# A decoder layer on one core: seven-product values, rows in place for one expert slot, and a reordered passage from attention to the experts

## The chip, the core and the metric

The kernel runs on one core of a Trainium2 chip. Five engines work side by side: TensorE (PE in the profile) multiplies matrices into PSUM, VectorE (DVE) and ScalarE (ACT) do elementwise work, GpSimd (POOL) does elementwise work and issues the indirect DMAs, SyncE (SP) issues most other DMAs. Each engine works through its own instructions in a fixed order and waits on semaphores for the others. The metric is device time in microseconds, lower is better.

## The reference

The input is x, 16 batches of 256 tokens of 256 features, and a context of 77 tokens for each batch. All is float32. Three residual steps, each followed by a layernorm, make up the layer:

```python
# 1. recurrent step: h = silu(causal conv of 4 taps (x @ in_w.T + in_b)), 512 features
xp  = h @ xp_w.T + xp_b
a   = exp(-exp(xp[..., :16]))
b   = silu(xp[..., 16:]) * sum(h, axis=-1, keepdims=True)
state_t = state_{t-1} * a_t + b_t                  # a scan over 256 tokens, 16 states
x   = layernorm(x + states @ out_w.T + out_b)

# 2. attention of x over [layernorm(context) ; layernorm(x)], 8 heads of 128
ln  = layernorm(x) * g + b
kv  = concat([layernorm(context) * g' + b', ln]) @ Wkv + bkv   # 333 rows, keys and values
out = softmax((ln @ Wq + bq) * 128**-0.5 @ k.T) @ v
x   = layernorm(x + out @ Wo + bo)

# 3. experts: each of 4096 tokens picks 2 of 8; an expert takes at most 512, first come first served
weights = softmax over the two best scores of x @ expert_embeddings.T
final[tokens of e] += weight * (relu(tokens @ W1[e].T) @ W2[e].T)
x   = layernorm(x + final)
```

## The kernel before, in words

**Loop over heads.** The main loop (L919 to L928) goes over 16 batches b of 8 heads h, and three heads are in work at once. `head_kq` makes keys (`pk`) and queries (`pq`) of the new head; `head_out` (L507) multiplies the turned weights of the head two back with the values (`po`); `head_softmax` (L473) makes the scores `s`, their negated maximum `nm` on DVE, `exp` on ACT and the scaled `pn` on DVE; `head_turn` (L492) turns `pn` of the head one back on PE (`pa`, `pb`) and copies it to `ptt`.

**Steps.** What belongs to other batches is hung on heads of this loop through a table, `steps[b, h]`, filled by `at` (L691 on). For batch b+1 these are the pieces of the recurrent step (`rec_in`, `rec_state`, `rec_add`, `rec_out`), its second layernorm and transposition (`prep_norm`, `prep_keys`) and its values (`prep_values`, L434). For batch b-1 they are the output product `project` (L526), the transposition `turn_tokens` (L559), scores and choice of experts (`score_experts`, `choose`), and `dispatch` (L635), which writes each token's row, with its weights and places, into a table of rows `xg` in device memory through indirect DMAs of POOL, two per 128 tokens. Batch 0's pieces run in a prologue ahead of the loop. A planner of the framework fixes the order of instructions on each engine from the code and the tile buffers, so the order on an engine is not that of the source alone.

**Values.** Values are 256 by 1024 from 256 by 256: four 128x512 results in PSUM, each of two accumulated 128x512 products (`pv`, L443), so eight products a batch; two results are copied by DVE (L451), two by ACT (L453). General PSUM tiles (`bank`, tag "mm": `pv`, `ph`, `pw`, `px`, `pt`, `pi`, `pf` and others) share two buffers; `pk`, `pq`, `pa` and `po` have one each.

**Layernorm.** `layernorm` (L135) takes statistics on DVE and the root on POOL as a power (`rsqrt`, L130). `again` (L151) derives the factor of a layernorm of an already normalised tensor by a short string on POOL (`u`, `u2`, `u3`, then `rsqrt`). Two such strings are in each batch: `rlz` for `prep_norm`'s `zl`, `rlo` for `settle`'s output `o`.

**Experts.** There are nine slots. Slot 0 is the first 512 rows of expert 0, slot 1 the rows of expert 0 that come from the last batch (256 places), slots 2 to 8 are experts 1 to 7 with 512 rows each. `Rows` (L774) loads a slot's rows `xe` from `xg` (L782) and works out on DVE, from `dw` (L787) on, each row's weight, where its token's other expert left a result, and where its output goes. `turn_rows` turns the rows on PE (`pe`), `first_product` makes `pi` and relu on ACT (L844), `second_product` makes `pf`, scaled by the weight on ACT and stored to `oe_d`. A token is completed by the later of its two slots: `gather` (L868) fetches the earlier result by indirect DMA, `finish` (L880) adds, normalises (root by POOL) and writes the output rows by indirect DMA (L903).

**The passage.** For the last batch, 15, nothing follows in the loop, so its project, router and dispatch stand behind the loop. Slot 0's rows need only batches up to 14, slot 1's need batch 15.

Of the kernel before, what the change touches and what calls it, by code (L numbers as in the profile page):

```python
# [10 lines left out]
F32 = mybir.dt.float32  # L11
# [7 lines left out]
P = 128  # L19
# [19 lines left out]
def decoder_layer(  # L39
# [66 lines left out]
    ebase_last = cpool.tile([P, GT, E], F32, tag="ebase_last", name="ebase_last")  # L106
# [8 lines left out]
    oob, tok1 = part[:, 0:1], part[:, 1:2]  # L115
    oobs = cpool.tile([P, 2], F32, tag="oobs", name="oobs")
# [63 lines left out]
    emb_s = wpool.tile([P, DC, E], F32, tag="emb", name="emb_s")  # L180

# [77 lines left out]
    zero = wpool.tile([P, 2 * DX], F32, tag="zero", name="zero")  # L259
    G.memset(zero, 0.0)  # L260

    def clear(i):

        xg_z = xg.rearrange("(i p r) d -> i p (r d)", p=P, r=2)
        for j in range(2 * i, min(2 * i + 2, xg_z.shape[0])):
            nc.sync.dma_start(xg_z[j], zero)
# [12 lines left out]
    def rec_in(pr, c):  # L279

        if c == 0:
            hss[pr] = aw.tile([P, NI, PT], F32, tag="hs", bufs=2, name=f"hs{pr}")
            sums[pr] = aw.tile([P, PT], F32, tag="sums", bufs=2, name=f"sums{pr}")
        ph = bank(f"ph{pr}_{c}")
        for k in range(DC):
            T.matmul(ph, lhsT=inw[:, k, c * P : (c + 1) * P], rhs=xTs[pr][:, k, :], start=(k == 0), stop=(k == DC - 1))  # L286
        hp = a2.tile([P, PB, KC - 1 + S], F32, tag="hp", name=f"hp{pr}_{c}")
        G.memset(hp[:, :, 0 : KC - 1], 0.0)
        A.activation(
            hp[:, :, KC - 1 :], ph.rearrange("p (b s) -> p b s", b=PB), AF.Identity, bias=inb[:, c : c + 1]  # L290
        )
        cv = a2.tile([P, PB, S], F32, tag="cv", name=f"cv{pr}_{c}")
        V.tensor_scalar(cv, hp[:, :, 0:S], cw[:, c, 0:1], cb[:, c : c + 1], ALU.mult, ALU.add)
        for k in range(1, KC):
            V.scalar_tensor_tensor(cv, hp[:, :, k : k + S], cw[:, c, k : k + 1], cv, ALU.mult, ALU.add)  # L295
        z = cv.rearrange("p b s -> p (b s)")
        th = a2.tile([P, PT], F32, tag="th", name=f"th{pr}_{c}")
        A.activation(th, z, AF.Tanh)
        V.scalar_tensor_tensor(hss[pr][:, c, :], th, 1.0, z, ALU.add, ALU.mult)
        if c > 0:  # L300
            G.tensor_tensor(sums[pr], hss[pr][:, 0, :] if c == 1 else sums[pr], hss[pr][:, c, :], ALU.add)

    def rec_state(first, last):
# [20 lines left out]
        for b, r in zip(members, rows):  # L324
            T.matmul(sg[r, 0:S], lhsT=half, rhs=sums[b // PB][:, tokens(b)], start=True, stop=True)
# [19 lines left out]
    def rec_add(b):  # L345

        pys = [bank(f"py{b + i}") for i in range(PB)]
        for h in range(2):
            for i in range(PB):
                ys, w = yss[b + i]  # L350
                T.matmul(
                    pys[i][:, h * D : (h + 1) * D], lhsT=ys[:, h * P : (h + 1) * P], rhs=w, start=True, stop=True
                )
        for i in range(PB):
            y = b2.tile([P, 2, D], F32, tag="ya", name=f"ya{b + i}")
            V.tensor_tensor(
                y.rearrange("p h d -> p (h d)"), pys[i], xts.pop(b + i).rearrange("p h d -> p (h d)"), ALU.add
            )
            ysums[b + i] = y
            if b + i + 2 < B:  # L360
                load_x(b + i + 2)

    def rec_out(b):

        xs[b] = xpool.tile([P, 2, DX], F32, tag="xs", name=f"xs{b}")
        stats[b] = layernorm(xs[b], ysums.pop(b), 2, P, f"a{b}")

# [4 lines left out]
    def context(t):  # L372

        rows = ctx_rows(t)
        zc = b2.tile([P, 1, D], F32, tag="zc", name=f"zc{t}")
        layernorm(zc, ctxs[t].unsqueeze(1), 1, rows, f"c{t}")
# [57 lines left out]
    def prep_values(b, n):  # L434

        if n == 0:
            vs[b] = b2.tile([P, 3, INNER], F32, tag="v", name=f"v{b}")
            nc.sync.dma_start(vs[b][0:M, 2, :], vc_d[b * M : (b + 1) * M, :])
        jc, half = divmod(n, 2)
        pv = bank(f"pv{b}_{n}")  # L440
        f0 = half * 512
        for k in range(DC):
            T.matmul(  # L443
                pv,
                lhsT=kvts[b][:, k, jc * P : (jc + 1) * P],
                rhs=wkv_s[:, k, INNER + f0 : INNER + f0 + 512],
                start=(k == 0),
                stop=(k == DC - 1),
            )
        if half == 0:  # L450
            V.tensor_copy(vs[b][:, jc, f0 : f0 + 512], pv)  # L451
        else:
            A.copy(vs[b][:, jc, f0 : f0 + 512], pv)  # L453

    kts, qts, pns, ptts = {}, {}, {}, {}
# [36 lines left out]
    def head_turn(b, h):  # L492

        pn = pns.pop((b, h))
        pt01 = bank(f"pa{b}_{h}", "pa", 1)
        pt2 = bank(f"pb{b}_{h}", "po", 1)
        for jc, (j0, jn) in enumerate(JCS):
            for ic in range(2):
                c0 = (jc % 2) * S + ic * P
                dst = pt01 if jc < 2 else pt2  # L500
                T.transpose(dst[0:jn, c0 : c0 + P], pn[:, ic, j0 : j0 + jn], ident)  # L501
        ptt = b2.tile([P, 3, S], F32, tag="ptt", name=f"ptt{b}_{h}")
        V.tensor_copy(ptt[:, 0:2, :], pt01.rearrange("p (j i) -> p j i", j=2))  # L503
        A.copy(ptt[0:M, 2, :], pt2[0:M, 0:S])  # L504
        ptts[b, h] = ptt

# [17 lines left out]
    pws, norms = {}, {}  # L524

    def project(b, i):  # L526

        ot = outs_t[b]
        if i == 0:
            pws[b] = bank(f"pw{b}")  # L530
        for h in range(H):
# [6 lines left out]
            )  # L538
        if i == 0:
            return  # L540
# [5 lines left out]
        norms[b] = layernorm(xs[b], y, 2, P, f"b{b}")  # L546

# [9 lines left out]
    x2s, lgs, chosen = {}, {}, {}  # L557

    def turn_tokens(b):  # L559
        x2s[b] = b1.tile([P, DC, S], F32, tag="x2", name=f"x2{b}")  # L560
# [74 lines left out]
    def dispatch(b):  # L635
# [13 lines left out]
        if b == B - 2:  # L649
            V.tensor_copy(ebase_last, ebase)  # L650
            for t in range(GT):
                V.tensor_scalar(
                    ebase_last[:, t, 0:1], carry[:, 0:1], -1.0, float(CAP), ALU.mult, ALU.add
                )
# [8 lines left out]
        V.tensor_tensor(place, cum, ebase_last if b == B - 1 else ebase, ALU.add)  # L663
# [26 lines left out]
    steps = {(b, h): [] for b in range(B) for h in range(H)}  # L690

    def at(b, h, f, *args):
        if 0 <= b < B:
            steps[b, h].append((f, args))
# [4 lines left out]
    for b in range(B):  # L699
        nb = b + 1  # L700
        new_pair = nb % PB == 0 and nb < B
        if b > 0:
            early = int(b == B - 1)
            at(b, 2, project, b - 1, 0)
            at(b, 3, project, b - 1, 1)
# [5 lines left out]
        if new_pair:  # L711
# [9 lines left out]
            for n, h in enumerate((4, 5, 6, 7)):  # L721
                at(b, h, prep_values, nb, n)
        elif nb < B:
            at(b, 0, prep_norm, nb)
            at(b, 0, prep_keys, nb)
            for n, h in enumerate((1, 4, 5, 6)):
                at(b, h, prep_values, nb, n)
# [4 lines left out]
    for nb in range(4, B, 4):  # L732
        for i in range(2):
            at(nb - 3 + i, 0, load_xT, nb // PB + i)
            for c in range(NI):
                at(nb - 3 + i, (1, 3, 5, 7)[c] if i == 0 else 4 + c, rec_in, nb // PB + i, c)
# [16 lines left out]
    for n in range(4):  # L753
        prep_values(0, n)
# [9 lines left out]
    e0 = e2 = es = None  # L764
# [7 lines left out]
    rows, xets = {}, {}  # L772

    class Rows:  # L774


        def __init__(self, e):
            expert, r0, self.n = SLOTS[e]
            code = float(E - expert)
            self.x = x = e0.tile([P, NS, DX], F32, tag="xe", bufs=3, name=f"xe{e}")  # L780
            x = x[:, 0 : self.n, :]
            nc.sync.dma_start(x, xg[r0 : r0 + self.n * P, :].rearrange("(s p) d -> p s d", p=P))  # L782
            narrow = lambda tag, e, dtype=F32: es.tile([P, NS], dtype, tag=tag, name=f"{tag}{e}")[:, 0 : self.n]
            first, token = x[:, :, D + 3], x[:, :, D + 2]

# [27 lines left out]
            self.to = narrow("to", e, I32)  # L813
            V.tensor_tensor(self.to, to, late, ALU.add)
# [31 lines left out]

    def second_product(e, it):
        y = e2.tile([P, NS, D], F32, tag="ye", name=f"ye{e}")
        w2 = w2_s[SLOTS[e][0]]
        for s in range(SLOTS[e][2]):  # L850
            po = bank(f"pf{e}_{s}")
            for f in range(NF):
# [6 lines left out]
                )  # L859
            A.activation(y[:, s, :], po[:, 0:D], AF.Copy, scale=rows[e].w[:, s : s + 1])  # L860
            if s % 2 == 1 and e < LAST:
# [4 lines left out]
    gs = {}  # L866

    def gather(e):  # L868
# [3 lines left out]
        for s in range(R.n):  # L872
            G.indirect_dma_start(
# [4 lines left out]
            )  # L878

    def finish(e, y):  # L880
        R, g = rows.pop(e), gs.pop(e, None)
# [3 lines left out]
        for a, z in [(0, 2), (2, 3), (3, 4)] if e == LAST else [(a, a + 2) for a in range(0, R.n, 2)]:  # L885
            for s in range(a, z):
                c = slice(s, s + 1)
                u = es.tile([P, D], F32, tag="u", name=f"ue{e}_{s}")
                V.tensor_tensor(u, R.x[:, s, 0:D], y[:, s, :], ALU.add)
                if e > 0:  # L890
                    V.scalar_tensor_tensor(u, g[:, s, :], R.joins[:, c], u, ALU.mult, ALU.add)
# [7 lines left out]
            r = rsqrt(v, n, P, f"e{e}_{a}")  # L899
# [15 lines left out]
    for i in range(len(heads) + 2):  # L915
# [3 lines left out]
        if i == len(heads) - 1:  # L919
            rows[0] = Rows(0)  # L920
# [8 lines left out]
        if 1 <= i <= len(heads):  # L929
            head_turn(*heads[i - 1])  # L930
# [8 lines left out]
    turn_rows(0)  # L939
# [4 lines left out]
    for e in range(LAST + 1):  # L944
        it = first_product(e)
        if e < LAST:
            rows[e + 1] = Rows(e + 1)
            turn_rows(e + 1)
        y = second_product(e, it)
        if e < LAST:  # L950
            gather(e + 1)
        finish(e, y)
# [52 lines left out]
```

## Time and profile before

| what | value |
|---|---|
| median of 3 runs | 1219.05 us (1216.42 to 1219.24) |
| the profiled execution's own time | 1219.84 us |
| its span, first to last instruction | 1218.1 us |
| mean granted TensorE clock | 0.988 |
| PE, DVE, ACT, POOL busy | 1169.6, 719.1, 480.5, 304.4 us |
| heads of attention | about 85 to 1060 us |
| last `pf` starts | 1198.40 us |
| last output store issued by POOL | 1213.94 us |

A line of the groups view gives line, engine and operation, output and input tiles, shape and count, then busy time in us and mean ns of one, then the idle time of that engine just before, with what ended it. In the timeline, a line begins with start and duration in us, and brackets at its end give idle time before and what released it. A line of the list of waits gives the waiting instruction, what it waited for, the total in us, how many times, and the longest. A line of the table by stretches gives the length, then PE, weight loads, DVE, ACT and POOL busy, the granted clock, the share of the DMA engines and GB/s. A float32 product shows as two matmul records.

### The profile page before, as it was taken

Reading aid. Unit: us, or ns where it says so; the run is one execution under the profiler, and the core shown is the slowest. Engines: PE = TensorE matmul, PEld = TensorE weight load, DVE = VectorE, ACT = ScalarE, POOL = GpSimd, SP = SyncE. Lnnn points to the kernel's source line nnn. Section 1 sums busy time; section 2 is a strip of 40 time slices with the busy share of each in tenths; the row PEclk is TensorE's granted clock in tenths of the full one; section 3 lists DMA queues with packets and bytes.
Section 4 is the critical chain, followed back from the end, with each engine's and each line's share of the span. In section 5 each row is a group of like instructions: output and inputs, shape, how many; then the busy total and the mean of one; then the engine's idle time right before and its main releaser. Section 6 shows DMA issues by size and latency. Waiting matters only on the chain.

```text
span 1218.1 us, 15598 instructions
## 1 busy us (share of the span) xinstructions
PE 1169.6 (96%) x5146; PEld 836.7 (69%) x5146; DVE 719.1 (59%) x2108; ACT 480.5 (39%) x1261; POOL 304.4 (25%) x516
## 2 busy tenths in 40 slices
PE   6799999999999999999999999999999999889995
PEld 2347676767777767677777676677787778756663
DVE  6525667485645675766465757754556464555654
ACT  2134534353434343543343444434443344323331
POOL 3300232122211321122112311321122112135666
PEclk9899999999999999999999999999999999999998
DMA  6740101001000100010001010000010000045762
GB/s 226 241 156 0 36 20 36 20 31 33 20 19 24 35 28 14 10 53 9 14 10 31 10 31 9 24 9 14 9 48 9 13 10 12 21 146 134 189 163 84
DMA packets 43321, 60.89 MB, mean 50 GB/s; under 512 B 7596, under 2 KB 31116, under 8 KB 43240
## 3 DMA queue, kind: packets, MB, share of 16 engines
q1 hardware_dynamic: 36376, 50.40, 13.0%
q0 software_dynamic: 6144, 9.48, 3.1%
q8 instruction: 41, 0.67, 0.2%
q14 instruction: 40, 0.33, 0.1%
q10 hardware_dynamic: 720, 0.01, 0.0%
HBM read 36.60 MB, written 30.78 MB: 55 GB/s over the span
## 4 chain that ended last, share of the span: by engine, by line
PE 83%; DVE 9%; POOL 3%; issue 2%; DMA 2%; ACT 1%; POOLq 0%; SPq 0%; DVEq 0%; ACTq 0%
PE po L514 12%; PE pk L463 11%; PE s L478 10%; PE pw L532 9%; PE pq L468 8%; PE pv L443 8%; PE pi L837 4%; PE pa L501 4%; PE ph L286 4%; PE pf L853 3%; PE pvc L395 3%; PE pb L501 2%; DVE cv L295 2%; PE pl L574 1%; POOL xg L679 1%
## 5 line engine op out<-in xcount | busy, mean ns | idle before, releaser
L480 DVE TENSOR_REDUCE nm<-s 128x2 f32<-128x666 f32 x128 | 108.5, 848 | 139.8 <-PE s L478 139.8
L514 PE MATMUL po<-ptt,v 128*128 128x256 f32 (+1 forms) x768 | 190.9, 382 | 0.0
L514 PEld LDWEIGHTS po<-ptt,v 128*128 128x128 f32 (+1 forms) x768 | 143.7, 191 | 52.7 <-issue 30.6
L463 PE MATMUL pk<-kvt,wkv_s 128*128 128x333 f32 x512 | 165.1, 444 | 0.0
L478 PE MATMUL s<-kt,qt 128*128 128x333 f32 x512 | 164.4, 442 | 0.0
L484 ACT ACTIVATE p<-s,nm 128x333 f32<-128x333 f32 x256 | 135.3, 535 | 38.0 <-DVE nm L480 37.1
L522 ACT ACTIVATE ot<-po,bkv_s 128x256 f32<-128x256 f32 x128 | 60.8, 475 | 211.8 <-PE po L514 211.1
L468 PE MATMUL pq<-kvt,wq_s 128*128 128x256 f32 x512 | 131.2, 378 | 0.0
L443 PE MATMUL pv<-wkv_s,kvt 128*128 128x512 f32 x256 | 121.5, 599 | 0.0
L504 ACT COPY ptt<-pb 77x256 f32<-77x256 f32 x128 | 47.1, 368 | 179.8 <-PE pb L501 179.8
L478 PEld LDWEIGHTS s<-kt,qt 128*128 128x128 f32 x512 | 96.4, 189 | 31.3 <-ACT qt L470 0.5
L468 PEld LDWEIGHTS pq<-kvt,wq_s 128*128 128x128 f32 x512 | 96.7, 189 | 30.6 <-issue 0.5
L532 PE MATMUL pw<-wo_s,ot 128*128 128x256 f32 x512 | 117.6, 382 | 0.0
L532 PEld LDWEIGHTS pw<-wo_s,ot 128*128 128x128 f32 x512 | 97.5, 191 | 13.4 <-ACT ot L522 0.2
L463 PEld LDWEIGHTS pk<-kvt,wkv_s 128*128 128x128 f32 x512 | 87.6, 191 | 23.0
L489 DVE TENSOR_SCALAR pn<-p,rs 128x333 f32<-128x333 f32 x256 | 92.3, 396 | 4.2
L501 PEld LDWEIGHTS pa<-ident,pn 128*128 128x128 f32 x512 | 63.7, 141 | 35.7 <-DVE pn L489 7.4
L543 POOL TENSOR_TENSOR xb<-xs,bo_s 128x256 f32<-128x256 f32 x32 | 21.2, 686 | 268.0 <-DVE yb L545 268.0
L679 POOL DMA_INDIRECT xg<-xs,sidx x64 | 66.4, 1037 | 86.2 <-DVE sidx L676 71.6
L503 DVE COPY ptt<-pa 128x512 f32<-128x512 f32 x128 | 87.3, 682 | 0.7 <-PE pa L501 0.7
L501 PE MATMUL pa<-ident,pn 128*128 128x128 f32 x512 | 77.9, 274 | 4.4 <-DVE pn L489 4.4
L295 DVE SCALAR_TENSOR_TENSOR cv<-hp,cw,cv 128x512 f32<-128x512 f32 x96 | 72.5, 757 | 1.6
(174 smaller groups left out, 1588.9 us busy)
## 6 DMA issues: line engine op xcount, KB each, us to landing
v<-vc SPq DMA_DIRECT2D x16, 308.0 KB
vc<-vc SPq DMA_DIRECT2D x9, 512.0 KB
xg<-zero SPq DMA_DIRECT2D x17, 262.0 KB, 4.8
xe<-xg SPq DMA_DIRECT2D x8, 524.0 KB, 4.6
xT<-in_xT SPq DMA_DIRECT2D x8, 512.0 KB, 3.7
xt<-in_x_in SPq DMA_DIRECT2D x16, 256.0 KB, 2.9
out<-o SPq DMA_DIRECT2D x16, 256.0 KB, 2.1
w<-in_w1T SPq DMA_DIRECT2D x8, 512.0 KB
```

What stands on the lines that cost most here:

```text
L295: V.scalar_tensor_tensor(cv, hp[:, :, k : k + S], cw[:, c, k : k + 1], cv, ALU.mult, ALU.add)
L443: T.matmul(pv, lhsT=kvts[b][:, k, jc * P : (jc + 1) * P], rhs=wkv_s[:, k, INNER + f0 : INNER + f0 + 512], start=(k == 0), stop=(k == DC - 1),)
L463: T.matmul(pk[:, 0:J], lhsT=wkv_s[:, k, f], rhs=kvt[:, k, :], start=(k == 0), stop=(k == DC - 1))
L468: T.matmul(pq[:, 0:S], lhsT=wq_s[:, k, f], rhs=kvt[:, k, 0:S], start=(k == 0), stop=(k == DC - 1))
L478: T.matmul(s[:, ic, 0:J], lhsT=qt[:, ic * P : (ic + 1) * P], rhs=kt, start=True, stop=True)
L480: V.tensor_reduce(nm, s[:, :, 0:J], AX.X, ALU.max, negate=True)
L484: A.activation(p[:, ic, :], s[:, ic, 0:J], AF.Exp, bias=nm[:, ic : ic + 1], accum_out=sm[:, ic : ic + 1])
L489: V.tensor_scalar(pn[:, ic, :], p[:, ic, :], rs[:, ic : ic + 1], None, ALU.mult)
L501: T.transpose(dst[0:jn, c0 : c0 + P], pn[:, ic, j0 : j0 + jn], ident)
L503: V.tensor_copy(ptt[:, 0:2, :], pt01.rearrange("p (j i) -> p j i", j=2))
L514: T.matmul(po[:, 0:S], lhsT=vs[b][0:jn, jc, h * DH : (h + 1) * DH], rhs=ptt[0:jn, jc, :], start=(jc == 0), stop=(jc == 2),)
L532: T.matmul(pws[b][:, i * D : (i + 1) * D], lhsT=ot[:, h, i * P : (i + 1) * P], rhs=wo_s[:, h, :], start=(h == 0), stop=(h == H - 1),)
```

## The change

- **Values by seven products.** The 2x2 block product (two token halves, two feature halves of the inner dimension, two halves of the values) is formed from seven 128x512 products. The weight side needs four sums, made once on DVE (`weight_sums`). The token side needs four 128x128 sums a batch, made on POOL (`prep_sums`, behind `prep_keys`). Steps come at three heads. At each a first product (at the first step two) goes into a bank, is copied or added into the values, and later in the same head, behind `head_turn`, a second product is accumulated into the same bank and evicted again (`late_steps`, `behind`). Per batch 2 copies on ACT and 5 adds on DVE stand for 2 and 2 copies.
- **Recurrent step.** For the first pair of batches the sum over features is accumulated by PE over four blocks, without the sums on POOL. `rec_add` adds into the loaded input tile; the next load of x is asked for in `rec_out`. The context is normalised in place. `rec_in` of later pairs hangs on other heads. Clearing `xg` takes 34 DMAs of half the size.
- **The passage.** In batch 15 the steps of batch 14 come one head earlier and both halves of its project at head 2. Slot 0's rows are asked for one head earlier, turned behind the last head's turn, and their DVE work (`read`) is placed behind the last copy of `head_turn`. project(15) uses two banks, and each half is normalised as it comes (`norm_half`).
- **Slot 1 in place.** All 256 tokens of batch 15 are slot 1, in their own order, whether they chose expert 0 or not. `dispatch` gives them their places through `slot_last`; `turn_tokens` writes their transposed rows straight to slot 1's tile; no rows are loaded back, turned or gathered for it. `read_last` gives weight 0 and no output to tokens that are not expert 0's.
- **Finishing.** Slots 1 to 8 take the root by a Sqrt on ACT, a reciprocal and a Newton step on DVE (`root`). In slot 8 the input and the gathered result are added up ahead of the second product, whose PSUM result is then scaled and added by DVE. The gather of slot 8 goes ahead of slot 7's stores on POOL.

```diff
-    def prep_values(b, n):
+    def weight_sums():
+        w = lambda k, half: wkv_s[:, k, INNER + half * 512 : INNER + (half + 1) * 512]
+        t = lambda i: wsum[:, i, :]
+        V.tensor_tensor(t(0), w(0, 1), w(0, 0), ALU.subtract)
...
+    def prep_sums(b):
+        x = lambda i, k: kvts[b][:, k, i * P : (i + 1) * P]
+        sums = b1.tile([P, 4, P], F32, tag="tsum", name=f"tsum{b}")
+        s = lambda i: sums[:, i, :]
+        G.tensor_tensor(s(0), x(1, 0), x(1, 1), ALU.add)
+        G.tensor_tensor(s(2), x(0, 0), x(1, 0), ALU.subtract)
+        G.tensor_tensor(s(1), s(0), x(0, 0), ALU.subtract)
+        G.tensor_tensor(s(3), x(0, 1), s(1), ALU.subtract)
+        tsums[b] = x(0, 0), x(0, 1), s(3), x(1, 1), s(0), s(1), s(2)
+    def prep_values(b, n, second):
...
+        if not second:
+            banks[b, n] = p = bank(f"pv{b}_{n}")
+            product(p, (1, 5, 7)[n], False)
+            if n == 0:
+                p6 = bank(f"pv6_{b}")
+                product(p6, 6, False)
+                A.copy(c(1, 0), p)
+                V.tensor_tensor(c(1, 0), c(1, 0), p6, ALU.add)
...
+            return
+        p = banks.pop((b, n))
+        product(p, (2, 3, 4)[n], True)
+        if n == 0:
+            A.copy(c(0, 0), p)
+        elif n == 1:
+            V.tensor_tensor(c(0, 1), c(1, 0), p, ALU.add)
         else:
-            A.copy(vs[b][:, jc, f0 : f0 + 512], pv)
+            V.tensor_tensor(c(1, 0), c(1, 0), p, ALU.add)
...
-            early = int(b == B - 1)
+            early = 2 * int(b == B - 1)
             at(b, 2, project, b - 1, 0)
-            at(b, 3, project, b - 1, 1)
+            at(b, 3 - early // 2, project, b - 1, 1)
...
             at(b, 3, prep_keys, nb)
-            for n, h in enumerate((4, 5, 6, 7)):
-                at(b, h, prep_values, nb, n)
+            at(b, 3, prep_sums, nb)
+            for n, h in enumerate((4, 6, 7)):
+                at(b, h, prep_values, nb, n, False)
+                behind(b, h, prep_values, nb, n, True)
...
+        first = ((1, 1), (1, 3), (1, 5), (1, 7)) if nb == 4 else ((0, 5), (0, 7), (1, 0), (1, 5))
+        at(nb - 4 + first[0][0], 0, load_xT, pr)
+        at(nb - 2, 0, load_xT, pr + 1)
+        for c, (b, h) in enumerate(first):
+            at(nb - 4 + b, h, rec_in, pr, c)
+        for c, h in enumerate((3, 4, 5, 7)):
+            at(nb - 2, h, rec_in, pr + 1, c)
...
+            if e == 1:
+                self.x = xs[B - 1]
+                return
...
+    def root(v, n, name):
+        q = es.tile([P, n], F32, tag="qe", name=f"qe{name}")
+        A.activation(q, v, AF.Sqrt)
+        i0 = es.tile([P, n], F32, tag="ie", name=f"ie{name}")
+        V.reciprocal(i0, q)
...
-        if i == len(heads) - 1:
+        if i == len(heads) - 2:
             rows[0] = Rows(0)
...
-            head_turn(*heads[i - 1])
+            turned = head_turn(*heads[i - 1])
+        if i < len(heads):
+            for f, args in late_steps[heads[i]]:
+                f(*args)
+        if i == len(heads) - 1:
+            turn_rows(0)
+        if i == len(heads):
+            with tc.issue_after(turned.ins):
+                rows[0].read(0)
...
         y = second_product(e, it)
-        if e < LAST:
-            gather(e + 1)
-        finish(e, y)
+        gathered = gather(e + 1) if 0 < e < LAST else None
+        if e == LAST - 1:
+            with tc.issue_after(gathered.ins):
+                finish(e, y)
+        else:
+            finish(e, y)
```

## The prediction

> **What bounds the kernel now.** I read the page's totals first, then its chain and its cost table.
>
> ```profile
> PE 1169.6 (96%) x5146; PEld 836.7 (69%) x5146; DVE 719.1 (59%) x2108; ACT 480.5 (39%) x1261; POOL 304.4 (25%) x516
> PE 83%; DVE 9%; POOL 3%; issue 2%; DMA 2%; ACT 1%; POOLq 0%; SPq 0%; DVEq 0%; ACTq 0%
> L443 PE MATMUL pv<-wkv_s,kvt 128*128 128x512 f32 x256 | 121.5, 599 | 0.0
> ```
>
> TensorE is busy for 96% of the span and owns 83% of the chain, and the value products that the change thins out are on it. How tight it is shows the list of what PE waited for, between 85 and 1040 us, which is nearly the whole attention loop:
>
> ```profile
> PE sg L325 <- POOL sums L301: 3.3, 4, 0.8
> PE ph L286 <- DVE x L566: 1.7, 3, 0.6
> PE px L315 <- DVE hs L299: 1.2, 3, 0.4
> PE pa L501 <- DVE pn L489: 0.6, 3, 0.2
> ```
>
> 6.8 us of waits in 955: PE work taken out there shortens the span, and anything that makes PE wait lengthens it. The 16 batches take 59.7 us each. Next the last of these waits, at batch 7, head 3, on three engines (start, duration, engine; in brackets the idle time before and its releaser). POOL first, then DVE, then PE:
>
> ```profile
> 552.80 0.71 POOL L132 TENSOR_TENSOR rb<-vb,nhalf 128x2 f32<-128x2 f32 x1 [0.64 <-DVE mva L141]
> 554.47 0.69 POOL L132 TENSOR_TENSOR ra<-va,nhalf 128x2 f32<-128x2 f32 x1
> 558.09 0.70 POOL L132 TENSOR_TENSOR rlz<-u3z,nhalf 128x2 f32<-128x2 f32 x1
> ```
>
> ```profile
> 558.83 0.35 DVE L415 TENSOR_SCALAR zl<-xs,rlz 128x256 f32<-128x256 f32 x1 [2.30 <-POOL rlz L132]
> ```
>
> ```profile
> 555.36 1.88 PE L443 MATMUL pv<-wkv_s,kvt 128*128 128x512 f32 x4
> 557.08 1.46 PE L514 MATMUL po<-ptt,v 128*128 128x256 f32 x6
> 559.87 0.84 PE L501 MATMUL pa<-ident,pn 128*128 128x128 f32 x4 [0.20 <-DVE pn L489]
> ```
>
> POOL works from 552.80 to 558.79 without a gap; DVE stands 2.30 us at zl for it; the softmax scaling pn is queued behind zl, and PE's pa waits for pn. The slack of this string of small operations is −0.2 us: it is already used up. Last, what PE waits for at the end of attention and in the first experts, and the granted clock there:
>
> ```profile
> PE pa L501 <- DVE pn L489: 3.8, 1, 3.8
> PE pe L822 <- DMA xe<-xg: 3.2, 1, 3.2
> ```
>
> ```profile
> 1060.00:1080.00 20.00, 18.90 (x74) 12.51 (x74) 7.51 (x31) 3.31 (x7) 2.94 (x7) 0.92 0.18 61
> 1080.00:1100.00 20.00, 16.69 (x66) 13.37 (x65) 11.46 (x71) 4.99 (x11) 11.70 (x12) 0.83 0.60 177
> ```
>
> ```profile
> 1090.89 1.12 PE L822 MATMUL pe<-ident,xe 128*128 128x128 f32 x4 [3.20 <-DMA xe<-xg]
> 1092.12 6.32 PE L837 MATMUL pi<-xet,w 128*128 128x256 f32 x16
> ```
>
> **The change, part by part.**
>
> *A, prologue.* Batch 0's values: seven products for eight, −0.9. Four weight sums on DVE, 128x512, about 0.65 each (the 128x512 copies took 0.68), in a stretch where PE already waits for DVE (6.5 us before pt at 48.7): 0 to +2.6, I take +1. The packed state sum gets 16 matmuls for 4, some +0.5 net of the 0.8 us wait on POOL that goes. Normalising the context in place removes one buffer's wait: 0 to −1, I take −0.8. Sum −0.2.
>
> *B, values in the loop.* The four passes above are two products and start 1.72 us before the next group: 0.86 us a product. 15 batches × 0.86 = −12.9.
>
> *C, the new wait.* The seven products need four 128x128 sums a batch on POOL. By the POOL rows of 1302 ns for 512 columns and 686 for 256, 128 columns cost 0.38, and 0.08 more where one uses the last. In the order of the changed kernel's instructions, in each odd batch b = 1, 3, ... 13 three of the four stand in POOL's queue between u3o and ra, so ra, uz, u2z, u3z, rlz come about 3 × 0.38 + 0.1 = 1.25 us later. Behind rlz wait DVE's two zl halves, and rs and pn of head 3 behind those, and PE's pa behind pn: the string above, with no slack. At b=3, 7, 11 (0.2 us short now) pa comes 1.45 late, at b=5, 9, whose filler ph moves elsewhere, about 1.4; b=13 has about 0.4 of slack, so 0.9; b=1 keeps its filler. 5 × 1.43 + 0.9 = 8.1, less the 0.6 that is there now: +7.5. If cover appears, +2; if the fourth sum slips in too, +10.
>
> *D, rec_in moved.* The 1.7 us of ph <- x go, as ph isn't next to turn_tokens any more: −1.7 (0 at worst). The sums waits stay.
>
> *E, small waits.* `choose` now follows the head's pn in DVE's order and its count product can come 0.2 late in some batches: +0.5. Evictions of the values wait on ACT and DVE (5 adds and 2 copies for 4 copies a batch), +0.2. Second products follow the first by po, s, pa and pb (1.30+1.12+0.65 = 3.07 us), more than an eviction of 0.6 to 1.5: nothing is late. The clears become 34 DMAs of half the size on SP, 17 more issues of under 0.5 us, all in batches 0 and 1, where SP has little else; load_x, moved to rec_out, lands 2.9 us after issue and has more than a batch. Both 0.
>
> *F, end of attention.* From the end of head 7's s (1051.9) to the end of the first slot's pf (1087.5) it is 35.6 us. The work in it, at full clock: pa, pb 0.65, two po 2.6, pw 6.9, transposes of tokens 0.9, router 1.4, pe 0.9, pi 7.0, pf 6.9 = 27.2. The rest is the 3.8 of pa (DVE stands at dw for the rows' DMA, ahead of pn), 1.1 of smaller waits and a halved clock. Now dw and what follows come after the last turn, and rows are asked for one head earlier (batch 14's dispatch also one earlier); project(15) is normalised in halves, each hidden by the first expert's products. I leave 1.6 us of waits: 28.8, so −6.8 (−4 to −8).
>
> *G, slot 1 in place.* No store and reload of the last batch's rows of expert 0 (now scatter to 1088.1, load 2.7), no pe(1). From the end of pf(0) to slot 2's pi it was 15.1 us. After: pi(1) and pf(1) at 256 columns each half of 6.9, pe(2) 0.87, = 7.8; slot 2's rows still wait for the last scatter and their own load: the counts' product to rows took 13.56 before (1044.05 to 1057.61), I take 12.9, and pe(2) is due 10.7 after it: +2.2. 10.0, so −5.1. [...] The row: 3.20 us of waiting, then 1.1 of transposes, and pi(1) took 6.32 for 3.45. My wait with its transposes is 3.1 us. By the row's own size it is warm, G −5.1; [...] pf(1) runs halved, G −1.7. I keep −5.1 and that end; −7 if rows come in time.
>
> *H, experts 2 to 8.* PE is full, 14.8 us each (7.0+0.9+6.9); root() puts a Sqrt on ACT, in order, ahead of relus that free PE's banks, waiting for DVE's ve. In slot 1 the first relu of slot 2 is some 0.5 late: +0.5. Later the rows are in time by 3 us or more: 0, up to +4. POOL, relieved of pow, only gains.
>
> *I, tail.*
>
> ```profile
> 1199.99 0.99 POOL L873 DMA_INDIRECT ge<-oe,at  x1 [0.30 <-issue]
> 1213.94 1.02 POOL L903 DMA_INDIRECT out<-oe,to  x1 [0.74 <-DVE oe L902]
> ```
>
> The last gather starts 8.6 us after pf(7) ended (1191.4), behind the stores of slot 7; now ahead of them, about 2.9 after. gather and input are added before the last product, so behind pf(8) (1205.4) remain an add from PSUM, statistics, Sqrt, four small DVE operations, scaling and a store: 0.5+0.4+0.2+0.2+0.3+0.6+0.4, with the handovers near 4.7 us to the last oe's end, which came 8.3 after: −3.5 (−1.5 to −5).
>
> Sum: −0.2 −12.9 +7.5 −1.7 +0.7 −6.8 −5.1 +0.5 −3.5 = −21.5. The profiled execution took 1219.84 (span 1218.1 and 1.7 around it): 1198.3. It lies 0.8 above the median of 1219.05, hence 1197.5.
>
> **The rivals.** *C is covered.* The string at rlz finds slack, as another order of POOL or the moved ph would give: the sum is −29, 1190. For: only 0.2 us is missing today. Against: POOL has no gap there, and three sums must go somewhere.
>
> *The expert stage turns on ACT and DVE.* Each root() holds the in-order ACT queue until DVE's statistics are there; 0.5 to 1 us in each of seven slots, plus a half-clock after G: +7 to +10, 1206. For: PE's two banks leave a relu 1.7 us. Against: ACT is busy only 6.7 of 20 us there. [...] the one load in the trace took 1.28. With a switch there and back for each of 16 roots it would be 41 us by the row [...]. The order of instructions has one added load, ahead of a wait of 2.5 us for slot 1's ve: 0 by the row[...].
>
> *Slower.* A bank held from first to second product: PE's general tiles have two, and the head between would find none. 45 second products in the loop; they decide the sign from 21.5/45 = 0.48 us each on; at 0.6 it is 1197.5 + 27 = 1224.5. For: at the first step two banks are taken at once. Against: the 3.07 us above.
>
> **How the numbers follow.** Forecast as summed 0.60; C covered 0.20; experts late 0.15; banks 0.05. The forecast's own ends (C from +2 to +10, G, I, F) make 1190 to 1204; the covered case and the late experts reach 1186 and 1207, where 0.2 is left out. About 0.3%, 3.7 us, is what a measurement tells from no change: faster 0.94, same 0.02, slower 0.04.
>
> **What would show it.** Right: value products 224 matmul records instead of 256; batch period near 59.3 with pa <- pn waits of 1 to 1.5 us at six heads 3 or 4; no pa wait over 1 us near 1040; pi(1) at 3.5 us; span end about 9 us after the last pf. Wrong, if pa <- pn stays below 2 us in all (then 1190), if waits for relus or pe appear in each slot, or if the second products show waits of their own.

## The result and the profile after

The changed kernel takes 1198.87 us (median of 4 runs, 1197.72 to 1201.09) against 1219.14 us (median of 4, 1216.42 to 1219.27): a ratio of 0.9841, 95% interval 0.9821 to 0.9861, or 20 us less. The profiled execution of the changed kernel took 1201.09 us with a span of 1199.3 us, the one before 1219.84 us with 1218.1, so the two traces differ by 18.8 us. The traced execution of the changed kernel is the slowest of its four.

To see where those went I cut both spans at the same five events on PE. The stages in us, worked out from the starts and durations of these instructions in the timeline of PE:

| stage | before | after | difference | predicted |
|---|---|---|---|---|
| prologue, to the first head's s | 87.40 | 92.37 | +4.97 | -0.2 (A) |
| loop, to the end of the last head's s | 964.74 | 956.64 | -8.10 | -6.4 (B to E) |
| to the end of pf of slot 0 | 35.55 | 27.47 | -8.08 | -6.8 (F) |
| to the start of pi of slot 2 | 14.91 | 9.69 | -5.22 | -5.1 (G) |
| to the end of pf of slot 8 | 102.87 | 104.83 | +1.96 | +0.5 (H) |
| to the end of the span | 12.63 | 8.30 | -4.33 | -3.5 (I) |

The total fits, and two of its terms do not: the prologue got longer by 5 us, and the loop hides two errors of mine that cancel. In the other runs that keep this prologue the first s comes at 89.25 to 92.65 us, so beside 87.40 its cost is 1.9 to 5.3 us, and this trace lies near the upper end. First the loop. The list of what PE waited for between 85 and 1030 us in the changed kernel:

```profile
PE po L564 <- DVE ptt L552: 6.3, 7, 1.2
PE sg L331 <- POOL sums L305: 2.9, 4, 0.8
PE pa L550 <- DVE pn L538: 2.6, 5, 0.5
PE ph L290 <- ACT v L496: 0.4, 1, 0.4
```

The waits of ph for x and of px for hs are gone, and a new one stands at the top. It comes seven times, once in each odd batch. Batch 7, head 3, is nearly at the same time as in the kernel before, and shows how. POOL in the changed kernel:

```profile
554.15 0.22 POOL L160 TENSOR_SCALAR u3o<-u2o 128x2 f32<-128x2 f32 x1
554.45 0.41 POOL L460 TENSOR_TENSOR tsum<-kvt 128x128 f32<-128x128 f32 x1
554.94 0.46 POOL L462 TENSOR_TENSOR tsum<-tsum,kvt 128x128 f32<-128x128 f32 x1
555.48 0.46 POOL L463 TENSOR_TENSOR tsum<-kvt,tsum 128x128 f32<-128x128 f32 x1
555.89 0.70 POOL L134 TENSOR_TENSOR ra<-va,nhalf 128x2 f32<-128x2 f32 x1
...
559.52 0.70 POOL L134 TENSOR_TENSOR rlz<-u3z,nhalf 128x2 f32<-128x2 f32 x1
```

DVE at the same place, first in the kernel before:

```profile
555.19 0.74 DVE L146 TENSOR_SCALAR xs<-ya,mva,ra 128x256 f32<-128x256 f32 x2
555.85 0.68 DVE L503 COPY ptt<-pa 128x512 f32<-128x512 f32 x1
```

and in the changed kernel:

```profile
556.63 0.74 DVE L148 TENSOR_SCALAR xs<-xt,mva,ra 128x256 f32<-128x256 f32 x2 [1.49 <-POOL ra L134]
557.28 0.68 DVE L552 COPY ptt<-pa 128x512 f32<-128x512 f32 x1
560.25 0.35 DVE L425 TENSOR_SCALAR zl<-xs,rlz 128x256 f32<-128x256 f32 x1 [2.29 <-POOL rlz L134]
```

And PE:

```profile
558.11 1.54 PE L564 MATMUL po<-ptt,v 128*128 128x256 f32 x6 [0.85 <-DVE ptt L552]
559.48 1.28 PE L527 MATMUL s<-kt,qt 128*128 128x333 f32 x4
561.29 0.85 PE L550 MATMUL pa<-ident,pn 128*128 128x128 f32 x4 [0.53 <-DVE pn L538]
```

Three sums on POOL put ra off from 554.47 to 555.89 and rlz from 558.09 to 559.52, by 1.42 and 1.43 us. DVE now waits for ra as well, at xs, and the copy ptt stands behind xs. So PE pays 0.85 us at po, which comes about 3 us ahead of pa, and another 0.53 at pa: 1.38 in all.

The passage from attention to the experts has lost most of its gaps, and the granted clock is 1.00 in both stretches, for 0.92 and 0.83 before (columns as before: length, the five engines' busy time, clock, DMA share, GB/s), with what PE waits for from 1025 us to the end:

```profile
1060.00:1080.00 20.00, 19.93 (x84) 13.93 (x82) 12.78 (x70) 5.56 (x13) 8.63 (x13) 1.00 0.45 142
1080.00:1100.00 20.00, 18.22 (x77) 13.21 (x78) 12.33 (x68) 7.62 (x15) 9.60 (x10) 1.00 0.62 174
```

```profile
PE pe L956 <- DMA xe<-xg: 1.8, 1, 1.8
PE pf L996 <- DVE ye L1004: 1.8, 1, 1.8
```

The first of the two waits is slot 2's rows (predicted 2.2). The second is new: the last product waits for a bank.

### The profile page after: what moved, and what is told of

Read it like the earlier page. It is cut to its first block, busy times and chain, and to the rows that moved or that the text cites. A ratio compares the mean times of both kernels' runs of the same rounds, so it can differ in the third digit from the quotient of the medians.

```text
span 1199.3 us, 15750 instructions
## 1 busy us (share of the span) xinstructions
PE 1152.6 (96%) x5134; PEld 827.8 (69%) x5134; DVE 748.6 (62%) x2226; ACT 485.4 (40%) x1273; POOL 312.3 (26%) x560
## 5 line engine op out<-in xcount | busy, mean ns | idle before, releaser
L512 PEld LDWEIGHTS pk<-kvt,wkv_s 128*128 128x128 f32 x512 | 91.1, 191 | 45.0 <-issue 22.0
L538 DVE TENSOR_SCALAR pn<-p,rs 128x333 f32<-128x333 f32 x256 | 97.8, 416 | 3.8
L514 ACT ACTIVATE kt<-pk,bkv_s 128x333 f32<-128x333 f32 x128 | 69.0, 539 | 19.9 <-PE pk L512 19.6
```

What stands on the lines that cost most here:

```text
L512: T.matmul(pk[:, 0:J], lhsT=wkv_s[:, k, f], rhs=kvt[:, k, :], start=(k == 0), stop=(k == DC - 1))
L514: A.activation(kt, pk[:, 0:J], AF.Identity, bias=bkv_s[:, h : h + 1])
L538: V.tensor_scalar(pn[:, ic, :], p[:, ic, :], rs[:, ic : ic + 1], None, ALU.mult)
```

## The experiments

All times below are medians; those of the kernel before, run beside each group, were 1218.64 to 1219.00. Stages are cut as in the table above. A median carries the prologue, whose length varies among executions (last section), so the stage that an edit aims at is given beside it. Theory: seven products are worth 0.86 us each batch, and the sums' place in POOL's queue gives part of it back. First rival: the waits belong to the split products and their evictions on DVE. For the passage and the tail the rivals were other parts of the same edit.

**Sums on DVE, and sums behind rlz.** Two ways to take the sums out of the way:

```diff
-        G.tensor_tensor(s(0), x(1, 0), x(1, 1), ALU.add)
+        V.tensor_tensor(s(0), x(1, 0), x(1, 1), ALU.add)
...
```

> The changed kernel with the four token-side sums of each batch on DVE instead of POOL; nothing else changed. Theory (the sums stand ahead of ra in POOL's queue and hold up xs, ptt, zl and pn on DVE): PE's waits for ptt and pn at the seven odd batches, 9.0 us in the changed kernel, fall below 2.5 us in all, and the time to 1190 to 1194. Rival (the waits come from the evictions of the split products on DVE): they stay near 9 us or grow by the added 60 operations on DVE, and the time is 1198 or more.

```diff
+        if b > 1 and b % 2 == 1:                      # in rec_out: rlz is made at once
+            r2s[b] = again(*stats.pop(b), f"z{b}")
...
+    def sums_behind(b):
+        with tc.issue_after(lasts[f"z{b + 1}"].ins):  # POOL: behind rlz
+            prep_sums(b)
...
-            at(b, 3, prep_sums, nb)
-            for n, h in enumerate((4, 6, 7)):
+            at(b, 4, sums_behind, nb)
+            for n, h in enumerate((5, 6, 7)):
```

> The changed kernel with the sums still on POOL, but in odd batches queued behind rlz (which is computed earlier for that), and the values of those batches at heads 5, 6 and 7 instead of 4, 6 and 7. Theory (it is the place in POOL's queue, not the engine): the 9.0 us of waits at odd batches go nearly all, time 1189 to 1192. Rival (evictions of the split products): the waits move with the products to heads 5 to 7 and the time stays at 1198.

On DVE: 1193.64 us, 5.2 less than the changed kernel; its loop takes 951.61 us for 956.64. Waits of 5.0 us remain (4.2 for ptt, 0.8 for pn), because the sums now stand on DVE ahead of ptt; more than the 2.5 I expected. Behind rlz: 1190.78 us (ratio to before 0.9776, 0.9760 to 0.9792), 8.1 less, with a loop of 947.81. What PE waited for between 95 and 1040 us in that run is down to this:

```profile
PE sg L335 <- POOL sums L309: 2.8, 4, 0.8
PE po L574 <- DVE ptt L562: 0.3, 1, 0.3
```

The split products and their evictions were all still there, so the rival falls. In batch 7 of that run POOL has ra and rlz ahead of the sums:

```profile
547.57 0.69 POOL L134 TENSOR_TENSOR ra<-va,nhalf 128x2 f32<-128x2 f32 x1 [0.93 <-DVE va L145]
...
549.86 0.69 POOL L164 TENSOR_TENSOR rlz<-u3z,nhalf 128x2 f32<-128x2 f32 x1
550.51 0.41 POOL L466 TENSOR_TENSOR tsum<-kvt 128x128 f32<-128x128 f32 x1
```

This edit also moves the values' first step from head 4 to head 5 and makes rlz earlier; the run alone doesn't part those from the order of the queue. The run on DVE, which moves neither, shows that 5.0 us of the loop go with the sums' leaving POOL.

**Eight products again.** Everything of the change kept but the values:

```diff
-                at(b, h, prep_values, nb, n, False)
-                behind(b, h, prep_values, nb, n, True)
+                at(b, h, prep_values, nb, n)          # prep_values, its steps and copies as before
...
-    wparts = weight_sums()
-    prep_sums(0)
```

> The changed kernel with the values of before (eight products, four copies, no sums on POOL or DVE), everything else of the change kept. Theory (a product is worth 0.86 us on PE, the sums cost 9.0 us by POOL's queue, and 1 to 2 us in the prologue): +12.9 - 9.0 - 1.5 = +2.4 us, 1200 to 1203. Rival (PE isn't the bound where the values are made, the seven products gained little): the time falls to about 1190.

1201.72 us, +2.85 against an expected +2.4. By the stages the agreement is in part chance. The loop is longer by 2.6 us (959.21), and that is what the seven products bring in it, net. The passage is longer by 2.4 us (12.04 to slot 2's pi, for 9.69): slot 2's rows came later in that execution (2.53 us of waiting, for 1.85), and slot 1's pf took 4.53 us for 3.62. Against these stand 3.6 us of a shorter prologue (first s at 88.81) and 0.8 in the last slots, so that the two traces differ by 0.6 us only. The length of single batches, from one head 0's s to the next in the timelines of PE, takes it apart:

| batch | before | eight products | changed | sums behind rlz |
|---|---|---|---|---|
| 3 | 58.80 | 58.75 | 59.35 | 57.88 |
| 7 | 58.79 | 58.75 | 59.35 | 57.87 |
| 12 | 56.05 | 56.04 | 55.19 | 55.18 |
| 13 | 58.28 | 58.23 | 58.82 | 57.88 |
| 14 | 56.04 | 56.04 | 55.18 | 55.18 |

In batches 12 and 14, which are even, seven products give 0.85 and 0.86 us, as the row of before said (0.86). In batches 3 and 7 the changed kernel is 0.6 us longer instead of 0.86 shorter. Over the seven odd batches the loss beside the eight-product kernel, 0.86 taken off, is 1.3 to 1.5 us each and 10.1 us in all. The eight-product loop itself is 5.5 us shorter than that of the kernel before (964.74): that is what the moved rec_in and the other edits in the loop bring, of which 3.1 us are waits that went (6.8 to 3.7 us); the other 2.4 are not assigned to a row.

**The prologue.** In the changed prologue PE reaches the first context products with a longer gap behind the fourth ph (16.41 to 21.99 us, before 17.32 to 19.95) with only small matmuls in it, and the products take longer:

```profile
18.56 0.44 PE L389 MATMUL pt<-ident,ctx 128*128 128x128 f32 x2 [2.16 <-ACT hp L293]
19.90 0.64 PE L319 MATMUL px<-hs,xpw 128*32 128x256 f32 x8 [0.90 <-ACT kvc L391]
21.00 1.06 PE L331 MATMUL sg<-hs,half 128*32 128x256 f32 x2 [0.46 <-ACT hp L293]
21.99 9.78 PE L405 MATMUL pvc<-wkv_s,kvc 128*128 128x512 f32 x16
```

Before they took 7.13. The granted clock is 0.50 from 22 to 26 us here and was 1.00 in the kernel before. Two experiments take edits of the prologue back, the first with one tile where the kernel before had two:

```diff
-        zc = ctxs[t].unsqueeze(1)
-        layernorm(zc, zc, 1, rows, f"c{t}")
+        zc = b2.tile([P, 1, D], F32, tag="zc", bufs=1, name=f"zc{t}")   # before: two buffers
+        layernorm(zc, ctxs[t].unsqueeze(1), 1, rows, f"c{t}")
```

> The changed kernel with the context normalised into a tile of its own again (one buffer), so that DVE's first convolution taps are no longer queued behind four normalisations. Theory (in the changed prologue PE stands still long enough ahead of the first context products that the clock halves for them: 7.8 to 9.8 us for 16 matmuls in four profiles against 7.13): PE reaches those products about 1.5 us earlier after its last large product, they take 7.1 to 7.5, the first scores come at 88 to 89.5 us instead of 92.4, and the time is 1196.5 to 1198. Rival (the longer prologue is the 16 matmuls of the state sum and DVE's weight sums): first scores stay at 91 to 92, time 1198 to 1199.

```diff
-        if c > 0 and pr > 0:
+        if c > 0:                        # POOL sums for pair 0 too, 4 matmuls for 16
             G.tensor_tensor(sums[pr], hss[pr][:, 0, :] if c == 1 else sums[pr], hss[pr][:, c, :], ALU.add)
```

> As the run before (context into its own tile), and the first pair's state sums on POOL again, so that 16 matmuls become 4. Theory (idle and clock, and the small matmuls lengthen the gap): first scores at 88 to 89, the first context products at 7.1, time 1195.5 to 1197.5. Rival (POOL's sums cost their 0.8 us wait back, and the gap stays): no better than the run before.

With its own tile for the context: 1191.89 us (0.9780, 0.9764 to 0.9796), 7.0 less than the changed kernel, where I had expected 1 to 2. The gap shrank to 3.7 us (16.47 to 20.18), the context products took 7.13, the first s came at 83.17. That accounts for 4.5 us up to the end of these products. Most of the rest is another wait, that neither kernel had lost: 6.5 us before the first zl is turned. With one tile the planner puts half of the small products py between the context products, and DVE gets at their sum earlier (38.03 us, for 45.70 in the changed kernel):

```profile
36.56 0.38 PE L389 MATMUL pt<-ident,zc 128*128 128x128 f32 x2
36.87 1.12 PE L363 MATMUL py<-outw,ys 32*128 32x256 f32 x4
37.93 3.70 PE L405 MATMUL pvc<-wkv_s,kvc 128*128 128x512 f32 x8
41.56 1.13 PE L363 MATMUL py<-outw,ys 32*128 32x256 f32 x4
44.30 1.07 PE L437 MATMUL pt<-ident,zl 128*128 128x128 f32 x4 [1.61 <-DVE zl L425]
```

In the changed kernel all of py stands at 44.54, behind the products, and zl's turn at 52.18 behind a wait of 6.51. Last, a wait of 1.68 us for a bank in batch 0's values is gone too.

With POOL's sums in addition: 1196.45 us, 4.6 more than with the tile alone, first s at 88.38. I had expected it to be the better of the two; its rival, POOL's sums bringing their wait back, came nearer. So beside a tile of its own for the context, the state sum by 16 matmuls is a gain, not a cost; in the changed kernel itself it was not tried alone. Of the 5.2 us between the first s of the two runs, 2.4 are eight context matmuls that took 6.10 us for 3.70, with a mean granted clock of 0.83 from 20 to 50 us (0.91 with the tile alone), behind waits of 2.29 us for hs and 1.08 for POOL's sums.

**The passage.** Slot 1's rows from the table again, and the order of before in the last batch:

```diff
-            if e == 1:
-                self.x = xs[B - 1]
-                return
...
-            if e > 0:
-                turn_rows(e + 1)
+            turn_rows(e + 1)
```

> The changed kernel, but slot 1's rows are loaded from the table of rows and turned on PE again, as before; its places, read-out and missing gather stay as in the changed kernel. Theory (the in-place rows save the store, load and turn of these rows ahead of slot 1's first product): a wait of 2 to 3.5 us for these rows and 0.9 us of turning come back ahead of slot 1, and the clock falls there; +4 to +6 us, 1203 to 1205. Rival (slot 2's rows arrive no earlier, so a wait just moves): +0.5 to +1.5 us, about 1200.

```diff
-            early = 2 * int(b == B - 1)
+            early = int(b == B - 1)
...
-        if i == len(heads) - 2:
+        if i == len(heads) - 1:
             rows[0] = Rows(0)
+            rows[0].read(0)
...
-        if i == len(heads) - 1:
-            turn_rows(0)
-        if i == len(heads):
-            with tc.issue_after(turned.ins):
-                rows[0].read(0)
```

> The changed kernel with the order of before in the last batch: batch 14's steps one head later, slot 0's rows asked for one head later and worked on by DVE at once, ahead of the last head's softmax scaling, and turned behind project(15). The halves of project(15) stay. Theory (DVE's work on slot 0's rows stood ahead of the last pn): PE's wait of 3 to 4 us for pn comes back, the clock falls below 1.0 after it, and with the turn moved it is +5 to +8 us, 1204 to 1207. Rival (most of the gain there came from the halves of project(15)): +1 to +3 us, about 1201.

With the reload 1203.60 us, +4.7. From the end of pf of slot 0 to slot 2's pi it is 15.05 us again, for 9.69, and slot 1's first product is slow, with a mean granted clock of 0.87 from 1080 to 1100 us (1.00 in the changed kernel), as it was in the kernel before (6.32 us, with a clock of 0.50 from 1091 to 1097):

```profile
1080.65 1.12 PE L953 MATMUL pe<-ident,xe 128*128 128x128 f32 x4 [4.26 <-DMA xe<-xg]
1081.86 5.41 PE L968 MATMUL pi<-xet,w 128*128 128x256 f32 x16
```

The changed kernel has 3.62 for that product.

With the old order in the last batch 1208.63 us, +9.8, more than expected. The stage to the end of pf of slot 0 is 35.96 us, as before the change (35.55); DVE stands at the rows again, and a wait and a lower clock follow:

```profile
1055.41 1.20 PE L550 MATMUL pa<-ident,pn 128*128 128x128 f32 x4 [3.04 <-DVE pn L538]
```

```profile
1040.00:1060.00 20.00, 16.96 (x76) 13.64 (x75) 9.52 (x46) 7.23 (x22) 4.04 (x4) 0.86 0.12 31
```

The halves of project(15) were kept in that run: without the order they bring nothing that this stage shows.

**The tail.** PSUM first in the last slot; the edge between gather and stores taken out; POOL's power for the roots:

```diff
-            for s in range(NS):
-                add_other(e, s, y[:, s, :], rows[e].x[:, s, 0:D])
...
-                V.scalar_tensor_tensor(y[:, s, :], po[:, 0:D], rows[e].w[:, s : s + 1], y[:, s, :], ALU.mult, ALU.add)
+                V.scalar_tensor_tensor(y[:, s, :], po[:, 0:D], rows[e].w[:, s : s + 1], rows[e].x[:, s, 0:D], ALU.mult, ALU.add)
+                add_other(e, s, y[:, s, :], y[:, s, :])
```

> The changed kernel, but in the last slot the PSUM result is scaled and added to the input first, and the gathered result is added afterwards (before: gathered result first, PSUM after). Theory (PE's 1.79 us wait in the last product is for the last gathered rows, which stand ahead of the PSUM reads on DVE): the wait goes, one DVE operation of 0.48 us is added per row group, net -0.8 to -1.6 us. Rival (the tail is paced by POOL's issues of stores, 1.28 us apart, so an earlier product gains nothing): no change.

```diff
-            with tc.issue_after(gathered.ins):
-                finish(e, y)
+            finish(e, y)
```

> The changed kernel without the edge that puts slot 7's stores behind slot 8's gather on POOL: two of the four stores then stand ahead of it. Theory (the gather waits for the landing of slot 7's results, 3.4 us behind its product, and POOL stands idle 5.75 us ahead of it, so that the edge gains nothing): within 0.8 us of 1198.9, gather issued at the same distance from the product. Rival (my step: the place in POOL's queue is worth up to 3.5 us): +2 us or more.

```diff
-            r = rsqrt(v, n, P, f"e{e}_{a}") if e == 0 else root(v, n, f"{e}_{a}")
+            r = rsqrt(v, n, P, f"e{e}_{a}")
```

> The changed kernel with the roots of slots 1 to 8 taken by POOL's power again (no Sqrt, reciprocal and Newton step); the last slot's order and all else as in the changed kernel. Theory (the root is on the path only in the tail, where three roots by POOL of 0.6 to 0.75 us with their handovers stand among its stores 1.28 us apart): +1.5 to +3.5 us, all behind the last product, 1200.5 to 1202.5. Rival (ACT's in-order Sqrt holds up relus in every slot): slots of 14.8 us get shorter without it and the time falls.

PSUM first: 1198.19 us. The intervals of the two kernels overlap, so the time alone says nothing; in its trace the wait of 1.79 us is gone, which in the changed kernel came from this order on DVE, the last gathered rows ahead of the read of PSUM:

```profile
1186.34 0.48 DVE L985 SCALAR_TENSOR_TENSOR ye<-ge,joins,xe 128x256 f32<-128x256 f32 x1 [1.62 <-DMA ge<-oe,at]
1186.74 0.48 DVE L1004 SCALAR_TENSOR_TENSOR ye<-pf,we,ye 128x256 f32<-128x256 f32 x1
```

With PSUM first, the stage to the end of the last pf is 102.76 us (for 104.83) and what follows is 8.98 (for 8.30), net -1.4.

Without the edge: 1200.29 us, its interval (0.9837 to 0.9873) overlaps too: the edge is worth 1.4 us or nothing. In its trace two stores stand ahead of the gather, which comes 4.1 us behind the product it needs, for 3.4; I had expected the same distance. The changed kernel shows why it can't be much. Its gather waits for slot 7's results to land, whatever stands in the queue:

```profile
1178.44 0.97 POOL L1031 DMA_INDIRECT ge<-oe,at  x1 [5.75 <-DMA oe<-ye]
...
1195.27 0.97 POOL L1064 DMA_INDIRECT out<-oe,to  x1 [0.30 <-issue]
```

With POOL's power 1204.49 us (1201.14 to 1208.67), +5.6, above what I expected and in another place: not behind the last product (7.55 us, for 8.30) but ahead of its end, where the stage is 110.40 us. The roots (0.57 to 0.76 us each) and their handovers (0.74 us ahead of a store) hold POOL, the planner sets the gather of slot 7 behind the stores of slot 6, the last slot's gather starts at 1179.31, 5.4 us behind the product it needs (3.4 in the changed kernel), and the last product waits for a bank:

```profile
1188.67 6.68 PE L996 MATMUL pf<-w,it 128*128 128x256 f32 x16 [4.30 <-DVE ye L1004]
```

So the root off POOL is worth its 5.6 us by what else POOL does. The rival (Sqrt holding up relus) falls for slots 2 to 7: they run at 14.8 us with the one root and with the other. PE waits for a relu once, 0.80 us at slot 2's pi in the run with the old order in the last batch; that slot 1's Sqrt held it up is not shown.

**Together.** Three edits that had gained or shortened a trace, on the changed kernel, and the same without the edge of the gather:

> The changed kernel with three of the edits together: sums queued behind rlz with the values of odd batches at heads 5, 6, 7; one tile for the normalised context; in the last slot PSUM first, the gathered rows after. If the three are independent: -8.1, -7.0 and -0.7, 1183 us. If the prologue's gain and the loop's waits are linked: 1186 to 1189.

> As the run before, and without the edge between slot 8's gather and slot 7's stores: if that edge gains nothing, within 0.8 us of the run before; if POOL's stores behind the last product pace the tail, 1 us less, since two stores leave the end of the queue.

1183.28 us (five runs, 1181.43 to 1183.80; ratio to before 0.9706, 0.9692 to 0.9719) and 1183.20 us. The sum of the three was 1183.1: they add up, stage by stage too (first s at 83.68, loop 947.76, to the end of the last pf 102.77), and this version beats both kernels, the changed one by 15.6 us. The edge is worth nothing there.

## Why the prediction was right

The forecast was 1197.5 us, measured 1198.87. That it came so near is in part luck: two steps failed, one in A and one in I, several sizes were off, and the errors cancel. By steps:

- **A, prologue (-0.2).** Failed. The trace has +5.0, of which about 2.7 are the context products at a lower clock (0.50 from 22 to 26 us; 9.78 for 7.13). I costed the weight sums and the state sum by row, and took the context's normalisation in place as a gain, the removal of one buffer's wait. It let the planner put four normalisations, three of them with a wait for POOL, ahead of DVE's first convolution, which started at 13.49 us instead of 10.97. Batch 0's values, that I had at -0.9, took 8.38 us (60.13 to 68.51) for 6.86, with the wait of 1.68 us for a bank in them. The state sum that I had at +0.5 is a gain of 4.6 us beside the tile of its own.
- **B, products (-12.9).** Right: 0.85 to 0.86 us a batch where nothing else acts.
- **C, sums in POOL's queue (+7.5).** Right in its place and cause, too small by a quarter: 10.1 us, and the run behind rlz took 8.8 off the loop. What I left out: xs waits for ra, and ptt is behind xs, so most of the wait comes at po and not at pa. The sign that I had named, waits of 1 to 1.5 us at pa in six heads, did not come (five of 0.53). And batch 1, which I called covered, pays too (1.24 us at po). A sum took 0.41 to 0.46 us where I took 0.38, and the three put ra off by 1.42 where I took 1.25.
- **D, E (-1.0).** Too small: -5.5. The waits of px for hs went too (1.2), and I had called the sums' waits unchanged. This and C's excess nearly cancel: -12.9 + 10.1 - 5.5 is -8.3, measured -8.1. (The batches take 60.3 us each, not 59.7: the window I divided was a little shorter than the loop.)
- **F, G (-6.8, -5.1).** Right: -8.1 and -5.2, with the wait for slot 2's rows at 1.85 for 2.2. I had left 1.6 us of waits in F; there are none of note. The clock stayed at 1.00 behind the gap of 2.8 us ahead of slot 1's pf (1079.94 to 1082.71, then 3.62 us for it), as I had taken it; behind the 5.5 us of the reload run slot 1's first product took 5.41 us for 3.62. In the run with eight products, where the rows came 0.7 us later than here, the gap was 4.2 us and pf took 4.53: the risk that I had named for G was near.
- **H, I (+0.5, -3.5).** The sum is right (-2.4 measured), one step failed: adding up ahead of the product puts the last gathered rows ahead of the PSUM reads in DVE's order, so PE waited 1.79 us for its bank. I had asked what is left behind the product, not what the product's own banks wait for. The gather came 3.4 us behind pf(7), not 2.9. The one added table load took 1.28 us at 1086.86, and nothing waited for it: the Sqrt behind it waits another 1.13 us for ve.

The rivals: "C is covered" is what the run behind rlz gives, 1190.8 against the 1190 worked out, though with the same cancelling errors in the other steps. The expert stage on ACT and DVE didn't come: slots stayed at 14.8 us. Nor did the held banks: no second product shows a wait in the loop, and ph waits once, for 0.4 us, for an eviction.

## What to carry to other kernels

An engine that is 25% busy can still be full where it counts: before work is put on it, look for the string of small operations there on which a busy engine waits in order, and place the new work behind that string. Where a wait is removed, ask which later instruction the planner will now put ahead of what. And let a read that frees a bank of PSUM not stand behind an operation that waits for a transfer: the read goes first, the late operand is added last (1.79 us of waiting here, 1.4 net in the trace, too little for the medians to tell).

## What the runs showed of the hardware that I had not expected

Seven profiles have the same prologue as the changed kernel up to the state, or nearly so, and their first s comes from 89.25 to 92.65 us. The first 16 context matmuls took 7.13 us in one of them, behind a gap without a large matmul of 4.1 us. In the other six the gaps were 5.3 to 6.6 us, and the matmuls took 7.70 to 9.78: for example 9.78 behind 5.6 us, 8.40 behind 5.3, 7.70 behind 6.2. Behind gaps of 2.6 us (the kernel before) and 3.7 us (the context in its own tile) they took 7.13. In these traces gaps of 5.3 us and more thus cost from 0.6 to 2.7 us, in no order of their length. The clock goes with it: from 20 to 50 us its mean was 0.85 in the profile with 9.78 us, 0.92 with 8.40 and 0.94 with 7.13. What sets the length behind such a gap is in none of these traces. The lower clock may also be some of the spread among executions of one kernel, about 3 us here: the slowest of the changed kernel's four has the lowest mean clock (0.991, the others 0.992 to 0.994). Only one execution of each kernel is traced, so this is not shown.
